# Layer 3 of a four-layer conditioned transformer: gelu read from PSUM, silu by tanh, statistics by chunk

## The chip, the cores and the metric

One Trainium2 chip; the kernel runs on one of its cores. The metric is the device time of one execution in microseconds (us), as the median of several runs. A profile is taken from one further execution; its own time and its span, from the first to the last instruction, stand in the table below.

## The reference: what is computed

The input is x of 4 batches, 512 tokens and 512 channels, with a condition vector per batch; all numbers are float32. Four layers follow each other. Layer 0 and layer 1 are attentions (layer 1 has an MLP with silu behind it), layer 2 is an attention with an MLP with gelu by tanh, and layer 3, which the change is about, is a layer of eight small experts:

```python
xr = x.reshape(Bx, Tx, 8, LATENT)                       # 8 experts of 64 channels
h = jnp.einsum('btel,elf->btef', xr, W1) + b1           # 64 -> 256
h = jax.nn.gelu(h, approximate=False)
y = jnp.einsum('btef,efl->btel', h, W2) + b2            # 256 -> 64
y = y.reshape(Bx, Tx, Dx)
eo = jax.nn.silu(emb) @ emb_W + emb_b
scale, shift = jnp.split(eo[:, None, :], 2, axis=-1)
hn = _layernorm(y, ln_g, ln_b) * (1.0 + scale) + shift
proj = jax.nn.silu(hn) @ out_W + out_b
return x + proj
```

## The kernel before

**Two streams.** The work of a batch is cut into stages: `a01` (layer 0 and the attention of layer 1), `m1` (the MLP of layer 1), `a2` (the attention of layer 2), `m2` (the MLP of layer 2 and the experts of layer 3). Two streams, A and M, each run a list of stages (lines 98 and 99), and their instructions are interleaved on the same engines, so that the full-size products of an MLP of one batch fill TensorE while the attention of another batch waits on softmax. The first two batches start together: batch 0's `a01` in stream M, batch 1's `a01` in stream A, with the small products of the conditioning between them. Batch 3 ends the program: its MLP of layer 2 runs in stream A, and its experts run in two halves of two token tiles, `half0` in stream M and `half1` in stream A, so `n` is 256 there and 512 elsewhere.

**The order is planned.** Every stage is a Python generator that yields between steps. The function `interleave` at the end of the kernel picks the stream whose next step is ready. What "ready" means comes from the class `Clocks` (line 161): a small model with a time for each engine's operation, in which tiles carry the time of their last use. Every operation is noted with its planned start, and the program is sorted by these starts before it is emitted. So an edit of one number in `Clocks` can move instructions anywhere in the program. `Clocks.matmul` (line 259) adds a fixed price when the tile shape of TensorE's array changes from one product to the next. `Until` (line 386) holds a step back until the banks it asks for are free and its operands are written.

**Engines.** TensorE multiplies (helper `mm`, line 354) and transposes against a unit matrix (helper `tr`, line 360). All operations of VectorE (DVE), ScalarE (ACT) and GpSimd (POOL) are noted by one line, 301, so the profile tells them apart by tile names. `evict` (line 376) copies a PSUM bank out on ScalarE or VectorE, whichever the plan says ends first. DMAs are issued on SyncE's queue.

**PSUM.** Eight banks: each stream has two single banks (`side.bank()`), and two tiles of two banks each (`two_banks()`, names `two`) serve the attention scores.

**The experts.** `experts` (line 1247) transposes x (`heads_T`), and then goes over four pairs of experts p with three helpers. `first(p)` computes the hidden values of two experts j, each in two halves f of 128 rows: for each f two products of 64 rows of the array (j = 0 and 1 in the upper and the lower half), (their two banks are the single banks of the stream in M, and a tile of `two` in `half1`), then an addition of b1 out of the bank (j = 0 on VectorE, j = 1 on ScalarE), then a yield; after both halves one gelu over all of it on ScalarE, in SBUF. `second(p)` contracts to 64 columns per expert and adds b2. `third(p)` transposes back to token order. The three are staggered: first(p + 1) stands ahead of second(p), and third(p - 1) behind it.

Then `norm` (line 630) takes bn_stats of 512 channels for each token tile, aggregates, raises to the power -1/2 on POOL, and scales. `turned` (line 653) transposes by chunk of 128 channels into a bank and applies gain and lift, even chunks on ScalarE and odd ones on VectorE. One silu goes over all four chunks in place. `by_token` (line 695) multiplies by out_W, through `product` (line 684), which yields after each of its four partial products so that other work can stand between them.

The tail of `experts` before, in its own lines:

```python
norm(y, y, 1e-5, tiles=tiles)
hT = side.late()
yield from turned(side, y, hT, b, coefs["gain"], coefs["lift"], tiles)
side.open = side.clear = side is sideM
scalar.activation(hT[:, :, lo : lo + n], hT[:, :, lo : lo + n], AF.Silu)
for t in tiles:
    ps = yield from by_token(side, t, hT, unit3)
```

**Activation tables.** Before a function of another table set runs on ScalarE, the program holds a table load; there are 39.

Of the kernel before, what the change touches and what calls it, by code (L numbers as in the profile page):

```python
# [15 lines left out]
ALU = mybir.AluOpType  # L16
# [144 lines left out]
class Clocks:  # L161
# [97 lines left out]
    def matmul(self, out, left, right, begins, emit, turn=False):  # L259

        tiling = tuple(32 if n <= 32 else 64 if n <= 64 else 128 for n in (left.shape[0], math.prod(left.shape[1:])))
        if turn:
            tiling = (128, 128)
        start = max(self.now, self.written(left) + self.WEIGHTS, self.written(right))
        if out.tile.fresh and out.tile.before:
            start = max(start, out.tile.before.last)
        n = math.prod(right.shape[1:])
        self.now = start + (0.00085 if turn else 0.001676) * n * tiling[0] * tiling[1] / 16384
        if tiling != self.tiling:
            self.now += 0.1  # L270
        self.tiling = tiling
        self.mark(left, self.now, False)
        self.mark(right, self.now, False)
        self.mark(out, self.now + self.TAIL + self.HOP, True)
        self.program.append((start, len(self.program), emit))
# [33 lines left out]
def cond_seq_kernel(ctx: ExitStack, tc: tile.TileContext, a: dict, out: bass.AP):  # L309
# [37 lines left out]
    def tiny(shape, tag):  # L347
        return clocks.tile(tag, 4, small, tuple(shape), tag, name(tag))
# [278 lines left out]
            gpsimd.tensor_tensor(d, u1, u2, ALU.add)  # L627


    def norm(n, src, eps, rms=False, tiles=range(NT)):  # L630

        mv, own = tiny([P, NT, 2], "mv"), slice(tiles[0], tiles[-1] + 1)
        for t in tiles:
            st = tiny([P, 6], "st")
            vector.bn_stats(st, src[:, t, :])
            vector.bn_aggr(mv[:, t, :], st)
        var = tiny([P, NT], "var")
        if rms:
            vector.tensor_tensor(var, mv[:, :, 0], mv[:, :, 0], ALU.mult)
            vector.scalar_tensor_tensor(var, var, eps, mv[:, :, 1], ALU.add, ALU.add)  # L640
        else:
            vector.tensor_scalar(var[:, own], mv[:, own, 1], eps, None, ALU.add)
        rstd = tiny([P, NT], "rstd")
        gpsimd.tensor_tensor(rstd[:, own], var[:, own], neg_half[:, own], ALU.pow)
        for t in tiles:
            if rms:
                vector.tensor_scalar(n[:, t, :], src[:, t, :], rstd[:, t : t + 1], None, ALU.mult)
            else:
                vector.tensor_scalar(
                    n[:, t, :], src[:, t, :], mv[:, t, 0:1], rstd[:, t : t + 1], ALU.subtract, ALU.mult  # L650
                )
# [32 lines left out]
    def product(side, left, right, n=NC):  # L684

        both = [(left(i), right(i)) for i in range(n)]
        yield Until(side.at, of=[x for pair in both for x in pair])
        p = side.bank()
        for i, (l, r) in enumerate(both):
            mm(p, lhsT=l, rhs=r, start=i == 0, stop=i == n - 1)  # L690
            if i < n - 1:
                yield PRODUCT
        return p
# [426 lines left out]
    def attention2(b, side):  # L1120
# [8 lines left out]
        for which, dst in (("q2", qT), ("k2", kT)):  # L1129
            unit = side.ring.take(which)  # L1130
            for t in range(NT):
                ps = yield from by_token(side, t, hT, unit)
                q, sq = side.t1(), side.t2()
                if which == "q2":
                    vector.tensor_tensor(q, ps, qb, ALU.add)
                else:
                    vector.tensor_copy(q, ps)
                scalar.activation(sq, q, AF.Square)
                ss, inv = tiny([P, 16], "ss"), tiny([P, 16], "inv16")
                vector.tensor_reduce(ss, sq.rearrange("p (h d) -> p h d", d=32), axis=AX.X, op=ALU.add)  # L1140

                vector.tensor_scalar(ss, ss, 1e-24, None, ALU.max)
                gpsimd.tensor_tensor(inv, ss, neg_half, ALU.pow)
                if which == "q2":
                    vector.tensor_tensor(inv, inv, mul, ALU.mult)
                qv = q.rearrange("p (h d) -> p h d", d=32)
                gpsimd.tensor_tensor(qv, qv, inv.unsqueeze(2).to_broadcast([P, 16, 32]), ALU.mult)
                yield PRODUCT
                if late:
                    yield from heads_T(side, *late)  # L1150
                late = (dst, t, q)
# [95 lines left out]
    def experts(b, side, tiles=range(NT)):  # L1247
# [11 lines left out]
        w1 = unit[:, 0:1024].rearrange("p (c f) -> p c f", f=256)  # L1259
        w2 = unit[:, 1024:2048].rearrange("p (e f l) -> p e f l", f=2, l=64)  # L1260
        y = side.n()

        def first(p):
            hid = side.hid()
            per = 4 // len(hid)

            def at(j, f):
                return hid[2 * j // per][:, (2 * j + f) % per, 0:n]

            for f in range(2):  # L1270
                yield Until(side.pair_at, of=[xT[:, p, lo : lo + n], w1])
                s = side.pair()
                for j in range(2):
                    r = slice(64 * j, 64 * j + 64)
                    mm(
                        s[j][:, 0:n], lhsT=w1[r, p, f * P : (f + 1) * P], rhs=xT[r, p, lo : lo + n],
                        start=True, stop=True,
                    )
                for j in range(2):
                    bias = V_B1 + 4 * p + 2 * j + f  # L1280
                    if j == 0:
                        vector.tensor_scalar(at(j, f), s[j][:, 0:n], vec[:, bias : bias + 1], None, ALU.add)
                    else:
                        scalar.activation(at(j, f), s[j][:, 0:n], AF.Identity, bias=vec[:, bias : bias + 1])
                yield 1.2 * n / S
            for h in hid:
                scalar.activation(h[:, :, 0:n], h[:, :, 0:n], AF.Gelu)
            return at

        def second(p, at):  # L1290
# [13 lines left out]
        def third(p, yT):  # L1304
            yield Until(side.at, of=[yT[:, 0:n]])
            ps = side.bank()
            for t in range(len(tiles)):
                tr(ps[:, t * P : (t + 1) * P], yT[:, t * P : (t + 1) * P], ident)
            evict(y[:, tiles[0] : tiles[-1] + 1, p * P : (p + 1) * P], ps[:, 0:n].rearrange("p (t n) -> p t n", n=P))
            yield 0.45 * n / S  # L1310

        hid = yield from first(0)
# [8 lines left out]
                t = tiles[p]  # L1321
                gpsimd.tensor_tensor(xs[b][:, t, :], xs[b][:, t, :], ob, ALU.add)
        yield from third(*late)
        norm(y, y, 1e-5, tiles=tiles)
        hT = side.late()
        yield from turned(side, y, hT, b, coefs["gain"], coefs["lift"], tiles)
        side.open = side.clear = side is sideM
        scalar.activation(hT[:, :, lo : lo + n], hT[:, :, lo : lo + n], AF.Silu)
        for t in tiles:
            ps = yield from by_token(side, t, hT, unit3)  # L1330
            if n < S:
# [16 lines left out]
    def conditioning(side):  # L1348
# [75 lines left out]
        vector.tensor_tensor(gain, e1, col(V_LNG), ALU.mult)  # L1424
        vector.tensor_tensor(lift, e1, col(V_LNB), ALU.mult)
        vector.tensor_tensor(lift, lift, coefs["e2"], ALU.add)
        yield 1.0
        load(bias2, a["bias"].rearrange("(t p) k -> p t k", p=P))
        ringM.load(2)
# [195 lines left out]
```

## Time and profile before

| what | us |
|---|---|
| median of 3 runs (2509.72 to 2513.07) | 2511.22 |
| the profiled execution, its own time | 2506.3 |
| its span, from the first instruction to the last | 2504.5 |
| TensorE (PE) busy | 2445.6 |
| VectorE (DVE) busy | 1178.7 |
| ScalarE (ACT) busy | 879.9 |
| GpSimd (POOL) busy | 735.2 |
| 39 table loads on ScalarE, 1283 ns each | 50.0 |

How to read the profile: names are `out<-in` by the program's tiles, with the buffer numbers left out. For TensorE `64*128 64x512` means 64 rows and 128 columns of the array in use, and an operand of 64 partitions and 512 columns. A float32 matmul leaves two records, one for each pass. "x4" is a count of instructions. "[1.95 <-ACT hid L301]" at the end of a row of the timeline is idle time of that engine and what ended it. PEclk is the granted TensorE clock, by 40 slices of the span on the page (tenths of full speed) and as a fraction in a row by window. `q0`, `k2` and the like in names of weights are the layer's projections; `wa` and `wm` are the weight rings of streams A and M, `wm_exp` the experts' weights, `wm_out` out_W; `two` and `bank` are PSUM.

### The profile page before, as it was taken

The numbers are of one execution on the slowest core, as the hardware profiler recorded it, in microseconds if no ns is written. First come the engines' busy times: TensorE is split into PE (matmuls) and PEld (weight loads), VectorE is DVE, ScalarE is ACT, GpSimd is POOL, SyncE is SP. The second block draws the span as 40 slices with busy tenths as digits, with TensorE's granted clock in tenths as the row PEclk, the third lists the DMA queues.
The fourth block names the chain that finished last, engine by engine and source line by source line (L and its number), as shares of the span: only waits on it lengthen the run. The fifth ranks groups of instructions, "written<-read, shape, count | busy, mean of one in ns | idle before, by whom it ended". The sixth has DMA issues, their size and how long they took to land.

```text
span 2504.5 us, 33302 instructions
## 1 busy us (share of the span) xinstructions
PE 2445.6 (98%) x12516; PEld 1248.2 (50%) x12516; DVE 1178.7 (47%) x3175; ACT 879.9 (35%) x2068; POOL 735.2 (29%) x921
## 2 busy tenths in 40 slices
PE   7889999999999999999999999999999999999997
PEld 3555565444554555554455455554455444554443
DVE  5574652224563363535555355453455332773233
ACT  2572542001452251424454044332355202660223
POOL 1342430004332233325322222433332205542221
PEclk9979999999999999999999999999999999999998
DMA  7200001221112111111110212112111221112210
GB/s 244 102 2 5 18 24 62 84 96 43 51 52 80 59 52 67 39 67 60 68 68 22 101 51 72 51 55 72 47 55 52 76 80 67 36 38 97 71 55 22
DMA packets 80145, 154.18 MB, mean 62 GB/s; under 512 B 3489, under 2 KB 6593, under 8 KB 79985
## 3 DMA queue, kind: packets, MB, share of 16 engines
q1 hardware_dynamic: 79376, 151.83, 17.5%
q8 instruction: 100, 1.64, 0.3%
q14 instruction: 61, 0.49, 0.1%
q0 software_dynamic: 176, 0.15, 0.0%
q10 hardware_dynamic: 432, 0.07, 0.0%
HBM read 147.83 MB, written 4.21 MB: 61 GB/s over the span
## 4 chain that ended last, share of the span: by engine, by line
PE 91%; DVE 3%; ACT 2%; issue 1%; DMA 1%; POOL 1%; ACTq 0%; POOLq 0%; DVEq 0%; SPq 0%
PE bank L354 74%; PE bank L360 12%; PE two L354 6%; ACT probs L301 1%; ACT wm L301 1%; DVE probs L301 1%; DMA wm_ada_t<-in_units 0%; POOL probs L301 0%; DVE neg L301 0%; DVE mx L301 0%; DMA wm_tw<-in_units 0%; DVE hid L301 0%; POOL inv L301 0%; DVE inv L301 0%; DMA wm_ada_s<-in_units 0%
## 5 line engine op out<-in xcount | busy, mean ns | idle before, releaser
L301 POOL TENSOR_SCALAR probs<-probs,inv 128x512 f32<-128x512 f32 (+4 forms) x544 | 318.2, 600 | 669.1 <-DVE inv L301 569.5
L301 ACT ACTIVATE probs<-probs,neg 128x512 f32<-128x512 f32 (+2 forms) x448 | 265.3, 593 | 244.1 <-DVE neg L301 243.9
L360 PEld LDWEIGHTS bank<-ident,probs 128*128 128x128 f32 (+2 forms) x1744 | 205.4, 143 | 166.8 <-issue 129.9
L360 PE MATMUL bank<-ident,probs 128*128 128x128 f32 (+2 forms) x1744 | 252.6, 279 | 8.1 <-POOL probs L301 3.6
L354 PE MATMUL bank<-mT,wm_gate 128*128 128x512 f32 x512 | 248.4, 596 | 0.0
L354 PE MATMUL bank<-mT,wm_up 128*128 128x512 f32 x512 | 246.5, 597 | 0.0
L354 PE MATMUL bank<-wm_down,hid 128*128 128x512 f32 x512 | 239.6, 596 | 0.7 <-DVE hid L301 0.7
L301 DVE CUSTOM_DVE_ANT_0 probs<-two,bias 128x512 f32<-128x512 f32 x256 | 166.8, 686 | 79.7 <-PE two L354 61.3
L354 PE MATMUL bank<-wm_fc,hid 128*128 128x512 f32 x384 | 187.1, 594 | 0.0
L354 PE MATMUL bank<-mT,wm_fc 128*128 128x512 f32 x384 | 181.6, 596 | 0.0
L301 ACT COPY pT<-bank 128x512 f32<-128x512 f32 (+3 forms) x240 | 133.9, 581 | 79.9 <-PE bank L360 72.2
L301 ACT ACTIVATE mt<-bank 128x512 f32<-128x512 f32 x64 | 37.8, 591 | 336.0 <-PE bank L354 336.0
L354 PE MATMUL bank<-wa_q,h 128*128 128x512 f32 x320 | 153.6, 596 | 2.0 <-DVE coef_e L301 1.2
L354 PE MATMUL two<-kT,nq 32*128 32x512 f32 (+5 forms) x1088 | 152.2, 544 | 2.4 <-DVE mx L301 2.3
L354 PEld LDWEIGHTS bank<-pT,v 128*32 128x32 f32 (+2 forms) x3488 | 109.5, 116 | 87.7 <-issue 30.9
L301 DVE TENSOR_TENSOR x<-x,bank 128x512 f32<-128x512 f32 x100 | 68.4, 684 | 177.9 <-PE bank L354 171.4
L354 PE MATMUL bank<-pT,v 128*32 128x128 f32 (+2 forms) x3488 | 145.2, 278 | 0.7 <-ACT pT L301 0.7
L354 PEld LDWEIGHTS bank<-wm_down,hid 128*128 128x128 f32 x512 | 91.7, 190 | 98.1 <-issue 96.2
L354 PEld LDWEIGHTS bank<-mT,wm_up 128*128 128x128 f32 x512 | 90.5, 190 | 95.6 <-issue 94.6
L301 DVE COPY pT<-bank 128x512 f32<-128x512 f32 (+2 forms) x199 | 131.4, 680 | 7.5 <-PE bank L360 6.8
L354 PEld LDWEIGHTS bank<-mT,wm_gate 128*128 128x128 f32 x512 | 90.1, 190 | 89.0 <-issue 88.5
L301 DVE RECIPROCAL inv<-total 128x2 f32<-128x2 f32 x320 | 52.9, 165 | 165.5 <-ACT probs L301 147.3
(221 smaller groups left out, 3392.9 us busy)
## 6 DMA issues: line engine op xcount, KB each, us to landing
wm_fc<-in_units SPq DMA_DIRECT2D x24, 1024.0 KB, 5.5
wm_gate<-in_units SPq DMA_DIRECT2D x16, 1024.0 KB, 5.4
wm_up<-in_units SPq DMA_DIRECT2D x16, 1024.0 KB, 5.7
wm_down<-in_units SPq DMA_DIRECT2D x16, 1024.0 KB, 5.6
wa_q<-in_units SPq DMA_DIRECT2D x10, 1024.0 KB, 5.4
wa_fc<-in_units SPq DMA_DIRECT2D x8, 1024.0 KB, 5.7
wa_o<-in_units SPq DMA_DIRECT2D x6, 1024.0 KB, 5.7
wa_k<-in_units SPq DMA_DIRECT2D x4, 1024.0 KB, 5.6
```

The source lines that it names most:

```text
L301: return call(*map(real, args), **{k: real(x) for k, x in kw.items()})
L354: latest[0] = nc.tensor.matmul(real(out), lhsT=real(lhsT), rhs=real(rhs), **kw)
L360: latest[0] = nc.tensor.transpose(real(out), real(src), unit)
```

## The change

Six edits, of which the first four are in the experts.

1. `first` asks for both pairs of banks of the ring `two` (one pair when n is 256), runs the four products of a pair of experts in one run with no yield between them, and applies gelu with the bias b1 straight from the banks, four ScalarE instructions that write SBUF. The separate additions and the gelu in place are gone.
2. bn_stats is taken for each chunk of 128 channels as soon as `third` has evicted it (16 per batch instead of 4); `norm` only aggregates.
3. `turned` is written out: for each chunk ScalarE computes tanh of the halved argument from the bank, VectorE computes the halved argument z from the same bank, and (tanh + 1) * z on VectorE is the silu. The gain and the lift are halved once in the conditioning. The silu over all chunks is gone.
4. A tile `stats` holds the statistics of a batch.
5. The copy of the key projection of layer 2 out of PSUM goes to `evict` instead of VectorE.
6. In the plan, a change of tile shape costs 0.2 instead of 0.1, and a bank that is being accumulated counts as taken until its last partial product is noted.

```diff
@@ -267,7 +267,7 @@
         n = math.prod(right.shape[1:])
         self.now = start + (0.00085 if turn else 0.001676) * n * tiling[0] * tiling[1] / 16384
         if tiling != self.tiling:
-            self.now += 0.1
+            self.now += 0.2
         self.tiling = tiling
         self.mark(left, self.now, False)
         self.mark(right, self.now, False)
@@ -627,12 +627,15 @@
             gpsimd.tensor_tensor(d, u1, u2, ALU.add)
 
 
-    def norm(n, src, eps, rms=False, tiles=range(NT)):
+    def norm(n, src, eps, rms=False, tiles=range(NT), stats=None):
 
         mv, own = tiny([P, NT, 2], "mv"), slice(tiles[0], tiles[-1] + 1)
         for t in tiles:
-            st = tiny([P, 6], "st")
-            vector.bn_stats(st, src[:, t, :])
+            if stats is None:
+                st = tiny([P, 6], "st")
+                vector.bn_stats(st, src[:, t, :])
+            else:
+                st = stats[:, t, :, :]
             vector.bn_aggr(mv[:, t, :], st)
         var = tiny([P, NT], "var")
         if rms:
@@ -686,7 +689,10 @@
         both = [(left(i), right(i)) for i in range(n)]
         yield Until(side.at, of=[x for pair in both for x in pair])
         p = side.bank()
+        p.tile.last = math.inf
         for i, (l, r) in enumerate(both):
+            if i == n - 1:
+                p.tile.last = 0.0
             mm(p, lhsT=l, rhs=r, start=i == 0, stop=i == n - 1)
             if i < n - 1:
                 yield PRODUCT
@@ -1134,7 +1140,7 @@
                 if which == "q2":
                     vector.tensor_tensor(q, ps, qb, ALU.add)
                 else:
-                    vector.tensor_copy(q, ps)
+                    evict(q, ps)
                 scalar.activation(sq, q, AF.Square)
                 ss, inv = tiny([P, 16], "ss"), tiny([P, 16], "inv16")
                 vector.tensor_reduce(ss, sq.rearrange("p (h d) -> p h d", d=32), axis=AX.X, op=ALU.add)
@@ -1259,6 +1265,9 @@
         w1 = unit[:, 0:1024].rearrange("p (c f) -> p c f", f=256)
         w2 = unit[:, 1024:2048].rearrange("p (e f l) -> p e f l", f=2, l=64)
         y = side.n()
+        if ("stats", b) not in shared:
+            shared["stats", b] = clocks.tile("stats", 1, small, (P, NT, NC, 6), "stats", name("stats"))
+        stats = shared["stats", b]
 
         def first(p):
             hid = side.hid()
@@ -1267,24 +1276,24 @@
             def at(j, f):
                 return hid[2 * j // per][:, (2 * j + f) % per, 0:n]
 
+            yield Until(lambda: clocks.free("two", 2, 2 if n == S else 1), of=[xT[:, p, lo : lo + n], w1])
+            banks = [two_banks() for _ in range(2 if n == S else 1)]
+
+            def bank(j, f):
+                return banks[f][:, j, :] if n == S else banks[0][:, j, f * n : (f + 1) * n]
+
             for f in range(2):
-                yield Until(side.pair_at, of=[xT[:, p, lo : lo + n], w1])
-                s = side.pair()
                 for j in range(2):
                     r = slice(64 * j, 64 * j + 64)
                     mm(
-                        s[j][:, 0:n], lhsT=w1[r, p, f * P : (f + 1) * P], rhs=xT[r, p, lo : lo + n],
+                        bank(j, f), lhsT=w1[r, p, f * P : (f + 1) * P], rhs=xT[r, p, lo : lo + n],
                         start=True, stop=True,
                     )
+            for f in range(2):
                 for j in range(2):
                     bias = V_B1 + 4 * p + 2 * j + f
-                    if j == 0:
-                        vector.tensor_scalar(at(j, f), s[j][:, 0:n], vec[:, bias : bias + 1], None, ALU.add)
-                    else:
-                        scalar.activation(at(j, f), s[j][:, 0:n], AF.Identity, bias=vec[:, bias : bias + 1])
-                yield 1.2 * n / S
-            for h in hid:
-                scalar.activation(h[:, :, 0:n], h[:, :, 0:n], AF.Gelu)
+                    scalar.activation(at(j, f), bank(j, f), AF.Gelu, bias=vec[:, bias : bias + 1])
+            yield 2.2 * n / S
             return at
 
         def second(p, at):
@@ -1307,6 +1316,8 @@
             for t in range(len(tiles)):
                 tr(ps[:, t * P : (t + 1) * P], yT[:, t * P : (t + 1) * P], ident)
             evict(y[:, tiles[0] : tiles[-1] + 1, p * P : (p + 1) * P], ps[:, 0:n].rearrange("p (t n) -> p t n", n=P))
+            for t in tiles:
+                vector.bn_stats(stats[:, t, p, :], y[:, t, p * P : (p + 1) * P])
             yield 0.45 * n / S
 
         hid = yield from first(0)
@@ -1321,11 +1332,21 @@
                 t = tiles[p]
                 gpsimd.tensor_tensor(xs[b][:, t, :], xs[b][:, t, :], ob, ALU.add)
         yield from third(*late)
-        norm(y, y, 1e-5, tiles=tiles)
+        norm(y, y, 1e-5, tiles=tiles, stats=stats)
         hT = side.late()
-        yield from turned(side, y, hT, b, coefs["gain"], coefs["lift"], tiles)
+
+        own = slice(lo, lo + n)
+        for c in range(NC):
+            yield Until(side.at, of=[y[:, t, c * P : (c + 1) * P] for t in tiles])
+            ps, h, z = side.bank()[:, 0:n], hT[:, c, own], side.t1()[:, 0:n]
+            for i, t in enumerate(tiles):
+                tr(ps[:, i * P : (i + 1) * P], y[:, t, c * P : (c + 1) * P], ident)
+            gain, lift = (coefs[x][:, c, b : b + 1] for x in ("gain", "lift"))
+            scalar.activation(h, ps, AF.Tanh, bias=lift, scale=gain)
+            vector.tensor_scalar(z, ps, gain, lift, ALU.mult, ALU.add)
+            vector.scalar_tensor_tensor(h, h, 1.0, z, ALU.add, ALU.mult)
+            yield 0.45 * len(tiles) / NT
         side.open = side.clear = side is sideM
-        scalar.activation(hT[:, :, lo : lo + n], hT[:, :, lo : lo + n], AF.Silu)
         for t in tiles:
             ps = yield from by_token(side, t, hT, unit3)
             if n < S:
@@ -1424,6 +1445,8 @@
         vector.tensor_tensor(gain, e1, col(V_LNG), ALU.mult)
         vector.tensor_tensor(lift, e1, col(V_LNB), ALU.mult)
         vector.tensor_tensor(lift, lift, coefs["e2"], ALU.add)
+        for x in (gain, lift):
+            vector.tensor_scalar(x, x, 0.5, None, ALU.mult)
         yield 1.0
         load(bias2, a["bias"].rearrange("(t p) k -> p t k", p=P))
         ringM.load(2)
```

## The prediction

> **What bounds the kernel now.** I read the page's busy times and its slices first, then the chain, then TensorE's groups of passes in order of time, and last the waits of the tail.
>
> ```profile
> PE 2445.6 (98%) x12516; PEld 1248.2 (50%) x12516; DVE 1178.7 (47%) x3175; ACT 879.9 (35%) x2068; POOL 735.2 (29%) x921
> PEclk9979999999999999999999999999999999999998
> PE 91%; DVE 3%; ACT 2%; issue 1%; DMA 1%; POOL 1%; ACTq 0%; POOLq 0%; DVEq 0%; SPq 0%
> ```
>
> TensorE is the bound nearly everywhere, so work taken from ScalarE or VectorE pays only where TensorE waits. "98% busy" isn't 98% at pace, though: a pass of 512 columns follows the last one after 0.429 us, a transpose's pass after 0.109 us. At that pace all passes of the trace add up to 2273 us of the 2504.5 us span; the other 231 us are the subject. From 400 to 2450 us they are almost all of one kind, changes of tile shape. TensorE's timeline in the experts of batch 0 (start, length, group):
>
> ```profile
> 1147.49 1.02 PE L354 MATMUL bank<-wa_q,h 128*128 128x512 f32 x2
> 1148.45 1.13 PE L354 MATMUL bank<-mT,wm_exp 64*128 64x512 f32 x4
> 1149.51 1.12 PE L354 MATMUL bank<-wa_q,h 128*128 128x512 f32 x2
> 1150.47 0.60 PE L360 MATMUL bank<-ident,t 128*128 128x128 f32 x4
> ```
>
> From start to start, two full passes at pace are 0.86 us, and so are the four half-height ones (two run side by side). The rows show 0.96, 1.06 and 0.96. Each step into or out of the 64-row tiling costs about 0.09 us at the change and 0.1 us in the first pass after. Summed over 400 to 2450 us: 462 changes without a wait lose 47.0 us at the change and 34.1 us just after, 0.176 us each.
>
> The two places that lose otherwise are the start (112 of the first 400 us) and the tail. Two stretches of the start, by window:
>
> ```profile
> core 0: us, PE busy (x) PEld busy (x) DVE busy (x) ACT busy (x) POOL busy (x), PEclk, DMA share, GB/s
> 80.60:117.70 37.10, 34.43 (x263) 20.11 (x265) 26.72 (x123) 23.18 (x83) 18.24 (x35) 1.00 0.33 115
> 117.70:189.60 71.90, 62.79 (x616) 40.75 (x613) 52.73 (x297) 50.01 (x203) 34.69 (x87) 0.76 0.01 2
> ```
>
> **The change, part by part.**
>
> **Changes of tile shape.** I counted them in both programs' TensorE order, which holds the same 7650 matmuls: 668 before, 621 after. The experts' four small products of a pair of experts now stand in a row instead of two and two with full-size work between: batches 0 and 1 go from 23 changes to 12 each, batch 2 from 24 to 13, the two halves of batch 3 from 35 to 20, all else from 563 to 564. 47 x 0.176 = **-8.3 us** (0.145 to 0.20 us each by the kind of change: -6.8 to -9.4).
>
> **The tail.** Its waits, then its end:
>
> ```profile
> PE bank L360 <- DVE nq L301: 3.9, 1, 3.9
> PE bank L354 <- ACT h L301: 3.1, 1, 3.1
> PE bank L354 <- ACT hid L301: 1.9, 1, 1.9
> ```
>
> ```profile
> 2471.59 4.85 PE L354 MATMUL bank<-wm_out,hid 128*128 128x512 f32 x7 [1.95 <-ACT hid L301]
> ...
> 2489.48 1.28 ACT L301 ACT_TABLE_LOAD   x1 [0.48 <-DVE h L301]
> 2490.77 1.06 ACT L301 ACTIVATE h<-h 128x1024 f32<-128x1024 f32 x1
> 2491.88 0.50 PEld L354 LDWEIGHTS bank<-wm_out,h 128*128 128x128 f32 x2 [3.46 <-ACT h L301]
> 2491.88 4.94 PE L354 MATMUL bank<-wm_out,h 128*128 128x512 f32 x7 [3.06 <-ACT h L301]
> ```
>
> A silu there costs a table load (1.28) and one pass over all four chunks (1.06), and the first output product waits for both. And after the wait the passes are slow: four at about 0.85 us, so 4.85 us for seven.
> (a) First half's output: 1.95 us of wait and 1.7 of slow passes now. In the new order four transposes of the next stage stand between the last chunk and this product, and each chunk is finished alone; I leave 0.5. About -3.2.
> (b) Small waits from 2454 to 2464 us, 1.3 us beyond the shape changes. In the new order the last half's experts come after that output, with nothing of another stage beside them. Sixteen gelus of 256 columns (0.47 each by the Identity row, some 0.40 apart) make about 7 us on ScalarE beside 9.4 us on TensorE; laid out by hand I find 0.6 of wait. About -0.7.
> (c) The last norm: from the last copy (2482.75) to the transposes (2486.21) 3.46 us, of it two statistics of 512 columns at 0.68. Afterwards only the last chunk's two of 128 stay there; no row has one that narrow, the 128-column copies are at 0.28. -0.8 (bounds: 0 and -1.4).
> (d) The last silu: from the first reading of a bank (2487.09) to the last pass's start (2500.10) 13.0 us now. Afterwards each chunk takes a tanh (0.56), a scaling (0.54), and a product on VectorE (half of the 0.69 of 512 columns). In the changed order the second reader of each bank waits for the first. With that the fourth chunk is done 4.75 us after the first reading; three products have run by then, five remain (4.3), and I leave 0.9 for slow passes (bounds 0 and 1.8): 9.5. -3.5.
> Sum of the tail **-8.2 us** (-4 to -11).
>
> [...]
>
> **Gaps in the experts of batches 0 and 1.** Now 0.85 and 0.68 us each. Afterwards the sixteen transposes of the norm stand in a row on two banks, each read by a scaling (0.80) and a tanh (0.78, from the two-scalar rows) in turn: the third waits about 1.4, the fourth 0.5. **+0.8 us** for both batches (-2 to +3).
>
> **The start.** The planner's price of a shape change goes from 0.1 to 0.2, and an unfinished bank counts as taken. Through this the order changes from the 17th matmul to about the 1166th. Before, from 80.6 to 117.7 us (the first row of the windows) batch 0's attention is alone beside batch 1's projections: 9 score units, 37.1 us for 28.0 at pace, 1.0 lost for each. From 117.7 to 189.6 (the row under it) both batches are in attention: 22 units, 71.9 us for 33.0, 1.77 lost for each, at a granted clock of 0.76. The new order has 13 units there instead of 22, the others beside projections: 9 x 0.77 = **-6.9 us**. The rate is borrowed and the DMA waits of the first 80 us may move: -15 to +10.
>
> **At no cost.** Gelu from the banks: per batch ScalarE has 16 x 0.68 = 10.9 us instead of 8 x 0.68 + 4 x 1.91 = 13.1, VectorE loses eight additions of 0.75 and gains two scalings of 0.80, four products of 0.69 and sixteen narrow statistics for four wide ones; both engines are under half busy and TensorE's queue covers it. Uncovered, a product waits 0.7 us per late gelu. Five table loads fewer (34 for 39) matter in the tail alone, counted above. Key copies of layer 2 move to ScalarE (16 of 0.58 for 0.69); TensorE waits 1.9 us in all on those tiles. POOL's and SP's instructions are as many as before.
>
> **Sum.** -8.3 - 8.2 + 0.8 - 6.9 = -22.6 us. The profiled execution took 2506.3 us (span 2504.5), so 2483.7; the shown runs' median is 2511.2, 4.9 above it, so **2488.6 us**.
>
> [...]
>
> **The rivals.**
> 1. *The start gives nothing*: its bound is VectorE's and ScalarE's latency (53 and 50 busy of 71.9 us), which no order shortens. 2488.6 + 6.9 = 2495.5. For it: both engines run in all phases; against: only the doubled phase has the low clock.
> 2. *The tail gives nothing*: the last half's gelus lie bare, as (b) fears, and take back what (a), (c) and (d) give. 2496.8. For it: the first half's output product hid them before; against: ScalarE's 7 us are less than TensorE's 9.4.
> 3. *Slower*: the first products now need both pairs of banks free, so each of the twelve of batches 0 to 2 waits for four gelus (4 x 0.68 = 2.7 us). All twelve bare add 32.8 us: 2521. It decides from 1.9 us of wait each (22.6 / 12). Against: in the new order a second product and four transposes, 2.3 us, mostly stand between.
> 4. *The start gains double*: 2481.7.
> That the change doesn't do what it says is no rival: the changed order already holds the 34 loads and the gelus that read the banks.
>
> **Chances.** Forecast 0.55, rival 1 0.18, rival 2 0.10, rival 3 0.07, rival 4 0.10. Range 2475 to 2502 leaves out rival 3 and the start's far end. By these, and with 0.2% (5 us) as about what a measurement of this kernel can tell: faster 0.87, same 0.06 (both 1 and 2 with the experts' gaps at their worst), slower 0.07.
>
> **What will show it.** 34 table loads; about 47 fewer shape changes; no wait over 0.6 us ahead of the first half's output; the last one near 1 us instead of 3.1; PEclk above 0.8 in the third and fourth slices. I am wrong if TensorE waits on gelu in the banks in batches 0 and 1, or if the first 370 us last longer.

## The result, and the profile after

The changed kernel takes **2502.22 us** (median of 7 runs, 2501.60 to 2507.27); beside it the kernel before took 2511.60 (7 runs, 2506.19 to 2513.47). The ratio is 0.9968, 95% interval 0.9956 to 0.9980: 5 to 11 us faster by the interval, 8.0 by the ratio, where 22.6 were forecast. The forecast of 2488.6 was missed, and its range, up to 2502, by 0.2 us.

The two profiled executions show less than the medians: 2506.3 before and 2503.99 after, 2.3 us apart. The kernel before varies with the granted clock of each run: over the 64 runs of it beside the experiments, the 33 at a mean clock of 0.985 or 0.986 average 2511.1 us and the 17 at 0.988 or 0.989 average 2506.8. Its profiled execution had 0.988; of the changed kernel's seven runs four had 0.992 and its profiled one 0.990. So the prediction's way to the median, "4.9 above it" for both, did not hold: traces are compared with traces below, times with times.

The page of the changed kernel, TensorE's total, its clock by slices and the chain:

```profile
PE 2435.3 (97%) x12516; PEld 1248.8 (50%) x12516; DVE 1178.4 (47%) x3198; ACT 866.6 (35%) x2101; POOL 734.7 (29%) x921
PEclk9989999999999999999999999999999999999998
PE 92%; DVE 4%; ACT 2%; DMA 1%; issue 1%; POOL 1%; ACTq 0%; POOLq 0%; DVEq 0%
```

TensorE is 10.3 us less busy, but the span is only 2.3 shorter: for 8 us more than before it now stands idle. The third slice shows the higher clock that was expected of the start (8 tenths for 7). The same part of the experts of batch 0, TensorE's timeline of the changed kernel:

```profile
1148.16 1.99 PE L354 MATMUL two<-mT,wm_exp 64*128 64x512 f32 x8
1150.08 1.94 PE L354 MATMUL bank<-hid,wm_exp 128*64 128x512 f32 x8
1151.95 0.66 PE L360 MATMUL bank<-ident,mt 128*128 128x128 f32 x4
```

Eight half-height passes in a row, 1.92 us from start to start, with one change of shape into them and one out. The tail by its waits (2428 to 2502 us, engine waited for, total, times, longest):

```profile
PE two L354 <- ACT hid L301: 3.1, 3, 1.9
PE bank L360 <- DVE nq L301: 2.9, 1, 2.9
PE bank L360 <- POOL x L301: 2.0, 1, 2.0
PE two L354 <- ACT pT L301: 1.8, 3, 0.6
```

The 3.1 us wait for the last silu and the 1.95 for the first half's are gone; in their place stand six waits of the products into `two` for a gelu, and one for POOL. The rows behind them, TensorE's and ScalarE's timeline of the changed kernel:

```profile
2430.74 1.13 PE L354 MATMUL two<-mT,wm_exp 64*128 64x256 f32 x6
2431.95 1.28 ACT L301 ACT_TABLE_LOAD   x1 [2.23 <-PE two L354]
2433.24 0.47 ACT L301 ACTIVATE hid<-two,vec 128x256 f32<-128x256 f32 x1
2433.77 1.56 PE L354 MATMUL two<-mT,wm_exp 64*128 64x256 f32 x10 [1.90 <-ACT hid L301]
...
2441.95 1.13 PE L354 MATMUL two<-mT,wm_exp 64*128 64x256 f32 x6
2443.70 0.70 PE L354 MATMUL two<-mT,wm_exp 64*128 64x256 f32 x2 [0.62 <-ACT hid L301]
2444.32 1.08 PE L354 MATMUL bank<-hid,wm_exp 128*64 128x256 f32 x8
...
2458.43 0.66 PE L360 MATMUL bank<-ident,x 128*128 128x128 f32 x4 [2.00 <-POOL x L301]
2458.92 6.58 PE L354 MATMUL bank<-wm_out,hid 128*128 128x512 f32 x11
...
2488.88 9.51 PE L354 MATMUL bank<-wm_out,h 128*128 128x512 f32 x16 [0.35 <-DVE t L301]
```

Four products are eight passes. The run is cut after six: three products, then one gelu, and only when that gelu has ended does the fourth product start. In the emitted program the fourth product is the only one of the four that carries a wait for a gelu of its own group. The wait reads 0.62 us, but from 2441.95 to the next group at 2444.32 it is 2.37 us for work that takes 1.07 uncut (below). The fourth product has also lost the neighbour that it ran side by side with: two passes side by side start 0.007 us apart, and its two passes now start alone, 0.32 us apart.

By number of the matmul in TensorE's order, counted from 0, both traces (us; a float32 product is two records, a transpose one):

| stretch | before | after | forecast of the difference |
|---|---|---|---|
| to 1775: the start | 549.7 | 543.5 | -6.9 |
| 1775 to 7377 without the experts: the body | 1635.7 | 1640.6 | 0 |
| experts of batches 0, 1 | 83.3, 83.7 | 82.1, 84.0 | -1.5 each |
| experts of batch 2 | 83.5 | 80.5 | -1.9 |
| 7519 to TensorE's end: the tail | 64.9 | 67.7 | -10.8 |

(The forecasts of the last three rows hold the shape changes at 0.176 us each, 11 for a batch and 15 for the two halves, and 0.4 us of gaps in each of batches 0 and 1. The expectations below call the 1775th matmul the 1806th; some of their lower marks stand elsewhere too, and the text gives what the records hold.) The start came near its forecast in the sum. The tail missed by 13.6 us, the body by 4.9.

**The theory** I then tested: the tail lost its gain because the halves put both halves of the experts' width into *one* buffer of two banks (`banks[0][:, j, f * n : ...]`, where batches 0 to 2 use two buffers), and a gelu that reads this buffer stands between the third and the fourth product in the program. The **rivals**: ScalarE's gelus are too slow for the halves in any order (rival 2 of the prediction), or the tail was lost by the silu and the statistics. For the body, that the price of 0.2 changes the order there too, against its being a consequence of the faster start.

### The profile page after: what moved, and what is told of

It is laid out like the page before. It is cut to its first block, busy times and chain, and to the rows that moved or that the text cites. A ratio compares the mean times of both kernels' runs of the same rounds, so it can differ in the third digit from the quotient of the medians.

```text
span 2502.2 us, 33351 instructions
## 1 busy us (share of the span) xinstructions
PE 2435.3 (97%) x12516; PEld 1248.8 (50%) x12516; DVE 1178.4 (47%) x3198; ACT 866.6 (35%) x2101; POOL 734.7 (29%) x921
## 4 chain that ended last, share of the span: by engine, by line
PE 92%; DVE 4%; ACT 2%; DMA 1%; issue 1%; POOL 1%; ACTq 0%; POOLq 0%; DVEq 0%
PE bank L354 73%; PE bank L360 11%; PE two L354 7%; ACT probs L301 1%; DVE probs L301 1%; ACT wm L301 1%; DVE neg L301 1%; DVE hid L301 0%; DVE pT L301 0%; ACT hid L301 0%; DMA wm_tw<-in_units 0%; DMA freq<-in_freq 0%; DMA wm_ada_t<-in_units 0%; DVE wm L301 0%; POOL probs L301 0%
## 5 line engine op out<-in xcount | busy, mean ns | idle before, releaser
L354 PE MATMUL bank<-mT,wm_gate 128*128 128x512 f32 x512 | 249.7, 597 | 0.0
L354 PE MATMUL bank<-mT,wm_up 128*128 128x512 f32 x512 | 246.5, 597 | 0.0
L354 PE MATMUL bank<-wm_down,hid 128*128 128x512 f32 x512 | 239.6, 596 | 0.7 <-DVE hid L301 0.7
L354 PE MATMUL bank<-wm_fc,hid 128*128 128x512 f32 x384 | 187.5, 594 | 0.0
L354 PE MATMUL bank<-mT,wm_fc 128*128 128x512 f32 x384 | 182.6, 597 | 0.0
L301 ACT COPY pT<-bank 128x512 f32<-128x512 f32 (+2 forms) x236 | 131.7, 580 | 79.7 <-PE bank L360 71.8
L354 PEld LDWEIGHTS bank<-pT,v 128*32 128x32 f32 (+2 forms) x3488 | 110.4, 116 | 95.4 <-issue 33.9
L354 PE MATMUL bank<-pT,v 128*32 128x128 f32 (+2 forms) x3488 | 146.1, 278 | 7.9 <-DVE pT L301 4.7
L354 PE MATMUL two<-kT,nq 32*128 32x512 f32 (+5 forms) x1088 | 151.3, 540 | 1.9 <-DVE mx L301 1.9
L354 PE MATMUL bank<-wa_q,h 128*128 128x512 f32 x320 | 152.0, 595 | 0.0
L354 PEld LDWEIGHTS bank<-wm_down,hid 128*128 128x128 f32 x512 | 91.7, 190 | 98.1 <-issue 96.2
L354 PEld LDWEIGHTS bank<-mT,wm_up 128*128 128x128 f32 x512 | 90.8, 190 | 96.7 <-issue 96.2
L354 PEld LDWEIGHTS bank<-mT,wm_gate 128*128 128x128 f32 x512 | 90.0, 190 | 90.8 <-issue 90.3
```

The lines of the kernel that those rows point to most:

```text
L301: return call(*map(real, args), **{k: real(x) for k, x in kw.items()})
L354: latest[0] = nc.tensor.matmul(real(out), lhsT=real(lhsT), rhs=real(rhs), **kw)
```

## The experiments

Ratios are to the kernel before, measured beside each experiment on the same chip. Its median there was 2508.8 to 2509.6 us, and 2511.6 beside the changed kernel, so kernels are better compared by their ratios than by their medians. Line numbers in some of their rows are two higher (L356 for L354).

### The planner's edits alone, and layer 3 alone

The kernel before with `self.now += 0.2` and the two lines on `p.tile.last`:

> The kernel before with the planner's two edits alone (price of a change of tile shape 0.2 instead of 0.1, an unfinished bank counted as taken); layer 3 is as before. Theory (the planner's order gains in the first 450 us what the pair of traces shows there, 6.2 us, and keeps it): 4 to 7 us below the kernel before, ratio 0.9972 to 0.9984, the 1806th matmul about 6 us earlier than before. Rival (the reordered start only moves waits about, and what it gains is given back by the end of the first attention phases of the other batches; the change's whole gain comes from layer 3): within 2 us of before, ratio 0.999 to 1.001.

The changed kernel without them:

> The changed kernel with the planner's two edits taken back; everything in layer 3 as changed. Theory (layer 3 gives some 4 us in the experts of batches 0 to 2 by fewer changes of tile shape and loses 2 to 3 us in the tail): 1 to 3 us below the kernel before, ratio 0.9988 to 0.9996, and 6 us above the changed kernel. Rival (all of the gain is layer 3's): 8 to 10 us below before, ratio about 0.997, as the changed kernel.

Planner alone: 2507.47 us, ratio 0.9991 (0.9981 to 1.0001), no difference that the interval bears out. Layer 3 alone: 2506.41, 0.9982 (0.9974 to 0.9991), 4.5 us below the kernel before: between the theory's 1 to 3 and the rival's 8 to 10, so neither held. In the trace the planner alone has the 1775th matmul 8.0 us earlier than before, but the experts of batch 2 begin 1.2 us *later* (2353.5, before 2352.3): the gain is given back in the body, as the rival said. Layer 3 alone makes the start longer: its experts of batch 0 begin at 1145.5 us, before at 1142.1, after at 1137.8. Its order differs from the one before from the 202nd to the 430th matmul, though no edit of layer 3 is used there; which of the small edits in the conditioning and the key copies moves the planner's choices was not tried.

### Only the bank, and the price only early

```diff
-            self.now += 0.2
+            self.now += 0.1
```

> The changed kernel with the price of a change of tile shape back at 0.1; the unfinished bank still counts as taken. In TensorE's order it differs from the kernel without both planner edits only from the 153rd to the 280th matmul. Theory (the price of 0.2 makes both the gain of the first 550 us and the loss of some 6 us spread over the rest; the bank edit makes little): as the kernel without both edits within 3 us, about 2506, the 1806th matmul at 554 to 560 us. Rival (the bank edit makes the start's gain and the price only the later loss): the 1806th matmul at 542 to 546 us and 2492 to 2495 in all.

2507.20 us, 0.9989 (0.9976 to 1.0002); the experts of batch 0 begin at 1145.2 us, 0.3 from the kernel without both edits. The bank edit makes neither the gain nor the loss; both come with the price (which was tried only together with the bank edit).

```diff
-            self.now += 0.2
+            self.now += 0.2 if self.now < 560.0 else 0.1
```

with the gelus moved as in the next experiment:

> The changed kernel with the gelus of the halves behind all four products, and the price of 0.2 only in the first 560 us of the planner's own clock, 0.1 after it. TensorE's order is then that of the changed kernel up to the 1938th matmul and that of the kernel without planner edits from there to the halves. Theory (the order made by the price of 0.2 costs some 6 us between the 1806th and the 7377th matmul by itself): that stretch takes about 1800.5 us instead of 1806.8, and the time is about 2488, 5 to 7 below the kernel that has only the gelus moved. Rival (the stretch is longer because the start was shorter, so that loads and the other batch's work come at other times, whatever the order): the stretch stays at 1805 to 1807 us and the time at 2493 to 2495.

2489.41 us, 0.9926 (0.9913 to 0.9940). That is 4.3 us below the next experiment's median, but only 2.3 by the ratios, and their intervals overlap. The traces are clearer: the spans are 2487.6 and 2491.9 us, and from the 1775th to the 7377th matmul it is 1802.4 us instead of 1806.9 (after: 1806.7, before: 1802.6). So the order by the price of 0.2 costs 4.3 us there by itself, and the rival (1805 to 1807 in any order) is out. One of the places, the waits of the changed kernel between 550 and 2352 us:

```profile
PE bank L360 <- ACT hid L301: 4.6, 4, 1.3
PE bank L354 <- ACT v L301: 1.8, 4, 0.5
```

The first row is the third and fourth bank of the norm's transposes in batches 0 and 1. The second is not there before, nor with the early price. It is of the kind that the tail has: products of the values' weights into one bank run 6 and 2 instead of 8, since an eviction of that bank got between them in the program.

### The gelus behind the products; two buffers

```diff
+            clocks.floor = clocks.now if n < S else 0.0
             for f in range(2):
                 for j in range(2):
...
                     scalar.activation(at(j, f), bank(j, f), AF.Gelu, bias=vec[:, bias : bias + 1])
+            clocks.floor = 0.0
```

and in `run`, `start = max(start, self.floor)`: the gelus of the halves come after the four products in the program; nothing else moves.

> The changed kernel; in the two halves of batch 3 the four gelus of a pair of experts are put behind all four small products in the program, instead of between the third and the fourth. TensorE's order and the buffers stay as they are. Theory (the fourth product waits for a gelu only because it comes behind it in the program and writes the same two-bank buffer, though not the same columns): the six waits of 1.90, 0.62, 0.62, 0.56, 0.62 and 0.62 us, 4.9 us in all, go, TensorE then waits for the gelus in no other place for more than 0.3 us each, and the time falls by 3 to 5 us against the changed kernel, to about 2498. Rival (ScalarE's gelus are too slow for the halves anyway, so the waits move to the products that read the gelus' output, and the bank's reader holds its writer back in any order): within 1 us of the changed kernel.

```diff
-                return banks[f][:, j, :] if n == S else banks[0][:, j, f * n : (f + 1) * n]
+                return banks[f][:, j, 0:n]
```

with two buffers asked for in the halves too:

> The changed kernel; in the halves of batch 3 the two halves of the experts' width go to two buffers of two banks each, as in batches 0 to 2, instead of sharing one. Theory (the wait is for the shared buffer): no product waits for a gelu inside its own four, the first wait of 1.90 us goes; but each group of four now needs both buffers, and so the last gelu of the group before, 1.6 us of gelus behind 1 us of products: of the 4.9 us of waits 2 to 4 go, and the time falls by 1.5 to 4 us against the changed kernel. Rival (the buffers don't matter, ScalarE is late): within 1 us of the changed kernel, the waits as long as before in other places.

Gelus moved: **2493.72 us**, 0.9935 (0.9922 to 0.9949). Two buffers: 2493.35, 0.9936 (0.9922 to 0.9949). Both are 8 to 9 us below the changed kernel (8.3 and 8.0 by the ratios), more than twice what I expected, and the rival (ScalarE too slow) is out: it has the same gelus. TensorE's timeline with the gelus moved:

```profile
2438.02 1.14 PE L356 MATMUL two<-mT,wm_exp 64*128 64x256 f32 x8
2439.09 1.08 PE L356 MATMUL bank<-hid,wm_exp 128*64 128x256 f32 x8
...
2453.19 0.66 PE L362 MATMUL bank<-ident,x 128*128 128x128 f32 x4 [2.00 <-POOL x L303]
2453.68 7.03 PE L356 MATMUL bank<-wm_out,hid 128*128 128x512 f32 x16
```

The same work takes 1.07 us from start to start instead of 2.37. Four such groups save 1.3 each; the first two of half 0, whose gelu had its table to load, 2.6 together, and the first two of half 1 1.25: 9.0 us for six waits that read 4.9. That is the part I had too small. The tail takes 57.4 us, 10.3 less than after, and the two traces reach the 7519th matmul within 0.1 us of each other. Of the 10.3, 1.7 are passes at half pace (0.85 us from start to start instead of 0.43) after the 2.00 us wait, which this execution does not have (more on this below).

### Old gelu, everywhere and in the halves

The old `first` (two products at a time, addition, gelu in place) put back in all batches, and with `if n < S:` in the halves alone:

> The changed kernel with the experts' first products and gelus as before, in all batches: two products at a time, the bias added on VectorE and ScalarE into SBUF, one gelu over all four chunks. Silu, statistics and planner as changed. Theory (the gelu part gives 3 to 5 us in batches 0 to 2 by fewer changes of tile shape, and costs 8 to 10 us in the halves): 4 to 7 us below the changed kernel, 2495 to 2498, with the tail from the 7519th matmul about 8 us shorter and the experts of batches 0 to 2 about 4 us longer. Rival (the gelu part is a gain in all places and the tail lost by the silu and the statistics): 3 to 8 us above the changed kernel, 2505 to 2510.

> The changed kernel with the experts' first products and gelus as before in the two halves of batch 3 alone. Theory (the shared two-bank buffer of the halves is what the tail lost by): 7 to 10 us below the changed kernel, 2492 to 2495, near the kernel with the gelus behind the products (its fewer changes of tile shape, 34 for 51 in batches 2 and 3, are worth up to 3 us more there). Rival (the tail lost by the silu and the statistics): within 2 us of the changed kernel.

Everywhere: 2499.93 us, 0.9968 (0.9955 to 0.9980). Halves alone: 2495.39, 0.9950 (0.9937 to 0.9962). The first expectation named 4 to 7 us below the changed kernel; the ratio is the changed kernel's own, so that is not shown. The second named 7 to 10: it is 6.8 by the medians and 4.5 by the ratios, short of that but beyond the rival's 2, and the trace's tail takes 60.7 us, 7.0 less than after. This splits the tail: silu and statistics -4.2 (64.9 to 60.7), gelu from one shared buffer +7.0 (to 67.7), gelu from the banks without the cut -3.3 (60.7 to 57.4). The 7.0 holds the 1.7 of passes at half pace that only the changed kernel's execution has there. The statistics by chunk were not run alone. In batches 0 to 2 the old gelu takes 84.2, 84.7 and 82.6 us for 82.1, 84.0 and 80.5.

### The old silu

> The changed kernel with the silu as before (scaling and shift by turns on ScalarE and VectorE, then one silu over four chunks, with its table load). Theory (the silu by tanh shortens the end after the last norm by 3 us or more, and costs up to 2 us in each of batches 0 and 1 by the bank's two readers): the tail from the 7519th matmul 2 to 4 us longer, the experts of batches 0 and 1 together 1 to 4 us shorter, the whole within 2 us of the changed kernel. Rival (the two readers cost more than the table load saves): 2 us or more below the changed kernel, with a tail no longer than its.

2503.38 us, 0.9974 (0.9964 to 0.9983): within 2 us of the changed kernel, as expected, but not by the expected sums. The end after the last norm (from its transposes to the end of TensorE) is 1.0 us longer, not 2 to 4; the tail as a whole is 1.3 *shorter*, because the first half has a wait for one gelu of 0.56 us where the changed kernel has 1.90 with a table load in it, and batch 1 is 1.7 shorter. Between the silu by tanh and the old one the times show no difference that the intervals bear out.

### The first half's output product earlier

`by_token` waits for the first chunk only, so the product stands ahead of the transposes that wait for POOL (on the kernel with gelus moved and the early price):

> The kernel with the gelus moved and the early price, and the first half's first output product planned as soon as its first chunk is finished instead of all four; in TensorE's order it then stands ahead of the four transposes that waited 2.0 us for POOL. Theory (that wait stands only because the transposes are first in the queue): the 2.0 us wait goes, a wait of 0.4 us or less for the fourth chunk is left, and the time falls by 1.5 to 2 us to about 2487.5. Rival (the product waits for the chunks as long as the transposes for POOL): no change, 2489.4.

2490.63 us, 0.9926 (0.9912 to 0.9940): no gain. The 2.0 us wait went; 1.09 (for the bank's second reader) and, behind the product, 0.68 (for the copy of the transposes) took its place, and the 16 passes took 8.8 us instead of 8.1.

### TensorE kept busy in the last waits

```diff
+        spare = two_banks()
+        for _ in range(20):
+            tr(spare[:, 0, 0:P], ident, ident)
```

> The kernel with the gelus moved and the early price, with 20 transposes of the identity into an unused bank ahead of the last transposes, in TensorE's wait for the last norm; they do no work that is used. Theory (the first passes of the last output run at half pace because TensorE stood still for 2.9 us before them): they fill 2.2 us of that wait, the slow passes go, the 16 passes take about 7 us instead of 8.9, and the time falls by 1.5 to 2 us to about 2487.5. Rival (the pace falls for another reason, or the transposes count for nothing because the waits of 0.8 and 0.4 us behind them are enough): the 16 passes stay near 8.9 us and the time at 2489.4 or 0.3 above.

2490.29 us, 0.9929 (0.9917 to 0.9942), the 16 passes 8.8 us: no gain. The rival's second form was right, the waits behind the first (1.02, 0.61 and 0.60 us, with 0.76 left of the first) were enough. So with 9, 5 and 5 more of them in these:

> The kernel with the gelus moved and the early price, and transposes of the identity into an unused bank in all four waits of the end: 20 in the wait for the norm, 9, 5 and 5 in those behind it (1.0, 0.6, 0.6 us). They do no work that is used. Theory (the passes go at half pace when TensorE has stood still for about 2 us in all of the last few us, in one wait or in several; 20 transposes in the first wait alone changed nothing since the three later waits remained): the 16 passes of the last output take about 7 us instead of 8.9, and the time falls by 1.5 to 2 us to about 2487.5. Rival (the half pace has nothing to do with TensorE standing still): 8.9 us again, and 2489.4 or a little above.

2488.36 us, 0.9917 (0.9904 to 0.9931), the lowest time of the study. The windows over the last output, first without the fillers, then with (window, its length, PE, PEld, DVE, ACT, POOL busy, granted clock, DMA share, GB/s):

```profile
2475.00:2479.00 4.00, 4.00 (x6) 1.69 (x7) 1.14 (x3) 0.11 (x1) 0.00 (x0) 0.56 0.00 0
```

```profile
2475.00:2479.00 4.00, 4.00 (x10) 1.82 (x10) 1.55 (x4) 0.00 (x0) 0.00 (x0) 1.00 0.00 0
```

And the 16 passes, without and with:

```profile
2474.85 8.93 PE L356 MATMUL bank<-wm_out,h 128*128 128x512 f32 x16 [0.35 <-DVE t L303]
```

```profile
2474.82 7.13 PE L356 MATMUL bank<-wm_out,h 128*128 128x512 f32 x16
```

Ten pass records in four microseconds instead of six. One execution could be luck, but the kernel with both changes of the next section has the same fillers and the same pace:

```profile
2478.02 7.13 PE L356 MATMUL bank<-wm_out,h 128*128 128x512 f32 x16
```

In nine traces without all the fillers (before, after and seven of the experiments) these 16 passes take 8.66 to 9.52 us. So at this place the half pace comes with TensorE's waits, behind several of them (2.94, 1.02, 0.36 and 0.35 us, granted clock 0.56) as behind those of the kernel before (3.86, 0.23 and 3.06 us, 0.50 over the next 3.4 us), and it is gone with fillers in all four, which leave 0.76 us of the first (granted clock 1.00). The trace shows 1.8 us; the times of the two kernels overlap (2488.45 to 2493.24 without, 2485.71 to 2489.44 with).

### The price for 200 us only, and both

> The kernel with the gelus moved, and the price of 0.2 only in the first 200 us of the planner's clock instead of 560. TensorE's order is the same up to the 918th matmul. Theory (the price gains in the phase where both batches are in attention and loses wherever a stage's products are alone beside one attention): up to the 902nd matmul as before, the stretch from the 1466th to the 1662nd 78.1 us as in the kernel before instead of 81.4, and that from the 902nd to the 1250th at most 79.7: 3 to 6 us less in all, 2483 to 2486. Rival (these stretches are longer because the start was faster, as the two batches then stand against each other in another way): 81.4 and 79.7 us again, 2489.

> Both together: the gelus moved, the price of 0.2 for 200 us only, and the transposes of the identity in the waits of the end. If both theories hold, the two gains add up, 4.5 to 8 us below the kernel with the gelus moved and the early price, 2482 to 2485; if neither does, 2489.

2489.07 us, 0.9922 (0.9908 to 0.9935): no gain that the intervals bear out. By TensorE's records the stretch from the 1250th to the 1662nd matmul fell from 136.4 to 133.1 us, its length in the kernel before, as the theory had it; but that from the 902nd to the 1250th rose from 82.4 to 86.8, and the gain is gone. Both together: 2490.75, 0.9928 (0.9915 to 0.9942), no better than either. A shorter stretch of one order is paid in the next; nothing here tells how to choose the price.

### The kernel before, profiled again

> The kernel before, profiled once more: its first profiled execution took 2506.3 us, 5 us less than its median. If executions differ in one place, the two profiles agree to 0.3 us in every stretch of the same order but that place; theory: it is in the first 200 us, where loads end the waits. Rival: the difference is spread evenly over the span.

2505.86 us in the profiled execution, again at a granted clock of 0.988, again below the median. From the 163rd matmul on no stretch between the marks used here differs by more than 0.4 us, and up to there it is 0.8 shorter. Where the other executions lose their 3 to 6 us is not shown by any profile.

## Why the prediction was wrong, step by step

- **The tail, "-8.2 us": this step failed.** Term (b), "laid out by hand I find 0.6 of wait", laid out the sixteen gelus of the last half as if each product waited only for its own bank, and for the first half the sum had no such term at all. In the program the fourth product waits for the first gelu, which reads the *other* bank of the same buffer: in this program the buffer counts, not the bank. That made six cuts, three in each half, 9.0 us. With (a) and (d) below this accounts for the miss of 13.6: 3.2 for (a), 8.4 here (9.0 for 0.6), 2.7 for (d), less about 0.7 that (c) and the shape changes gave beyond their forecast. The order with its waits was there to be read before the run; I read the order of the matmuls and not their waits. Whether TensorE could write one bank of this buffer while ScalarE reads the other was not tried.
- Term (a), "I leave 0.5. About -3.2": 0. The four transposes that I counted as cover were themselves waiting 2.00 us for POOL's last addition, and 1.7 us of slow passes followed, as before.
- Term (c), -0.8: right. From the last copy (2482.19) to the transposes (2484.72) 2.5 us instead of 3.46, with two statistics in 0.49.
- Term (d), -3.5: mis-sized. From the first reading to the last pass's start 12.2 us, not 9.5. The chunks were ready as forecast, but all transposes stand ahead of the first product, which began 3.3 us after the first reading, about 1.1 later than the sum needs, and the slow passes took 2.5 us for the 0.9 that I left.
- **The body, at 0: failed by 4.9 us.** "The order changes from the 17th matmul to about the 1166th" was wrong. The price moves where attention is cut all through the kernel, with as many shape changes outside the experts (353) but other waits; the early price took 4.3 of it back.
- **The start, -6.9: right in the sum**, -6.2, but in part by luck: from the 163rd to the 902nd matmul it is -12.9, nearly twice what the rate and the count of units gave, and later stretches and first loads take 6.7 back.
- **Shape changes, "-8.3", and gaps, "+0.8":** for batches 0 to 2 -3.9 measured for -5.0. Without TensorE's waits of over 0.2 us the experts of batches 0, 1 and 2 are 2.3, 2.4 and 2.4 us shorter than with the old layer 3 under the same planner prices (planner alone), for eleven changes each: 0.20 to 0.22 us a change, the upper end of what was forecast. The gaps were the mis-sized term: in each of batches 0 and 1 they went from 1.5 to 2.6 us (the third and fourth bank at 1.28 and 1.04, where 1.4 and 0.5 were forecast, and one of 0.29), +2.2 for both. Batch 1 loses another 1.5 to the price (against layer 3 alone, waits left out).
- Rival 2 named the right place and the right sign; its reason, ScalarE's time, was wrong. Rival 3 did not occur: no product waits on a gelu in batches 0 to 2.
- **What was to show it:** 34 table loads, yes; 47 fewer shape changes in the program's order, yes; the clock in the third slice, yes; "no wait over 0.6 us ahead of the first half's output", no; the last wait, 0.35 instead of about 1.

With the gelus moved and the price early the time is 2489.4, within 1 us of the forecast 2488.6. The agreement is partly chance: the terms (a) and (d) are missing from it, the median's 4.9 us too, and the kernel before ran at 2508.9 beside it. By its ratio it is 18.6 us faster than the kernel before (15 to 22), of the 22.6 forecast.

## What to carry to other kernels

When an edit puts more into one on-chip buffer, read the waits in the changed program and not only the order: a reader of one part of a buffer can hold back a writer of another (six waits of 0.56 to 1.90 us), and placing the reads behind the last write was worth 8.3 us here. A short wait in the middle of a side-by-side group cost more here than the trace's idle time says (1.3 us for 0.62). A cover that itself waits (2.00 us) is no cover, and a planner's price works everywhere (4.3 us in the body), not only where one looks.

## What the runs showed of the hardware that I had not expected

The same wait of 2.00 us ahead of the same 16 passes was followed by 1.7 us of half pace in the changed kernel and by none with the gelus moved. The windows behind the wait, first the changed kernel, then with the gelus moved (columns as above; the granted clock is the third figure from the end, 0.60 and 1.00):

```profile
2458.90:2463.20 4.30, 4.30 (x9) 1.76 (x8) 0.63 (x2) 0.59 (x1) 0.00 (x0) 0.60 0.00 0
```

```profile
2453.70:2458.00 4.30, 4.30 (x13) 1.91 (x12) 1.28 (x3) 0.59 (x1) 0.00 (x0) 1.00 0.00 0
```

So a wait of this length can halve the pace or leave it; what decides between the two is not shown by any run here.

At the end of the program four waits of 0.35 to 2.94 us with transposes between them were followed by the half pace, and with the first filled to 0.76 the other three of 0.60 to 1.02 still were (8.83 us for the 16 passes, 7.13 with fillers in all four). In the kernel before 1.95 us of idle ahead of 2471.59 were too (granted clock 0.53 over the next 3.4 us).
